# The first graph's column blocks and x ahead of the keys and the row loads in a four-layer graph network

## The chip, the cores and the metric

The kernel runs on one core of a Trainium2 chip. The metric is the device time of one execution, in microseconds (us), as the median of several executions. Five engines run side by side, each through its own list of instructions: TensorE (PE, matmuls and transposes), VectorE (DVE), ScalarE (ACT), GpSimd (POOL) and SyncE (SP, which here only issues transfers). ACT and POOL issue transfers as well. Engines wait for each other, and for transfers, by semaphores.

## The reference

Sixteen graphs of 1024 nodes with 64 features each go through four layers. `adj` is a dense 1024 x 1024 matrix for each graph with few non-zero entries. Each layer norms x, applies ReLU, and adds its result to x.

```python
# x (16, 1024, 64), adj (16, 1024, 1024), nodemask (16, 1024)
h = maximum(layernorm(x), 0)
x = x + einsum('bnf,of->bno', einsum('bnm,bmf->bnf', adj, h), L0_W)
h = maximum(layernorm(x), 0)
x = x + gru(relu(adj @ mlp(h)), h)                 # layer 1: message, then gates
h = maximum(layernorm(x), 0)
T1 = adj @ h; T2 = 2 * adj @ T1 - h                # layer 2: Chebyshev
x = x + (K0 * h + K1 * T1 + K2 * T2) @ weight + bias
h = maximum(layernorm(x), 0)
# layer 3: neighbours of each node from adj > 0, some dropped where there are more than ten;
# for each feature the 0.25, 0.5 and 0.75 quantiles over the neighbours, weighted 0.25, 0.5, 0.25
x = x + mlp2(h + quantiles(h, neighbours(adj))) * nodemask
```

## The kernel before, in words

Every graph passes these stages, each written as a Python generator that yields instructions:

- `transposing` (lines 798 to 832) loads the adjacency matrix by column blocks (128 columns, 512 KB each, eight a graph), transposes them on TensorE against the identity matrix and has ACT copy the result to a tile `AT`.
- `layers` (line 851) loads x of its graph into `pay`, and computes layers 0 to 2, with products `AT,nodes` on TensorE. Two such chains run at once, one for even graphs and one for odd. `norm` (line 834) is the layer norm: DVE sums a row (`st`), ACT squares (`sq`) and takes the root (`sd`), DVE forms `ri` and `off`, ACT writes the normed rows (`nodes`). At the end, `table` and `rows` are stored to DRAM (line 619).
- `lists` (line 633), called from `listing`, finds each node's neighbours from the matrix's rows, also eight loads of 512 KB a graph. For each it forms a `key` on DVE from the row and the constant `keys`, which lies in the tile `c16` (550 KB, loaded once from `half`), and takes the largest by MAX8 instructions.
- `gathering` and `gathers` fetch the neighbours' features by indirect transfers of POOL, 80 for a graph (line 613), and at the end those of nodes with long lists, which `longest` numbers (`whom`).
- `quantiling` sorts what was gathered on DVE, and `dense` is the last small network.

A planner, `Weave` (line 311), orders all of this when the program is built. It asks each generator for its next instruction, keeps a model of durations, takes the engine that can start earliest, and on it the instruction of lowest key among those that could start within 0.1 us. A bare number that a generator yields sets its key from there on. So x of graph 0 has key -1.0 (line 1039), and rows of graph 0 have key 0.0. The planned order is then fixed for every engine and for SP's issues. Where the model shows a gap of more than 0.5 us on TensorE, the planner puts fillers in it: matmuls of `ones` (line 567), whose result nobody reads. `leash` makes a gather wait for instructions of TensorE that the model has finished by then.

Ahead of the planned part stands a set-up in `Fast.__init__`: constants `c32` (with the identity matrix), the weights, small biases by POOL, and `wg`, two transposes of weights that DVE copies out of PSUM at line 535. The banks that the planned matmuls write are allotted after this set-up's PSUM pool.

For graph 0, blocks 2 to 7 and rows 2 to 5 go to parts of the tiles `G`, which are otherwise used by the gathers (`self.early`), so that all eight blocks and six rows have a place at the start.

Of the kernel before, what the change touches and what calls it, by code (L numbers as in the profile page):

```python
# [454 lines left out]
class Fast:  # L455
# [4 lines left out]
    def __init__(self, tc, half, whole, weights):  # L460
        self.tc, self.nc = tc, tc.nc
        (W0, W1, b1, W2, b2, Wih, bih, Whh, bhh, Wc, K, bc, M1, mb1, M2, mb2) = weights
        nc = self.nc
# [4 lines left out]
        def fixed(name, shape, dtype):  # L468
            return cp.tile(shape, dtype, name=name)
# [6 lines left out]
        c16 = fixed("c16", [P, half.shape[1]], F16)  # L476
# [15 lines left out]
        with tc.tile_pool(name="fsetup_ps", bufs=1, space=PSUM) as spp:  # L492
            passing = self.small("h1", (P, 512))
            w0 = passing[0:C, 0:C]
            nc.scalar.dma_start(w0, W0)
            whi = passing[0:96, C:C + 2 * P].rearrange("p (a g) -> p a g", a=2)
            nc.scalar.dma_start(whi[:, :, 0:C], Whh.rearrange("(a p) h -> p a h", p=96))
            nc.scalar.dma_start(whi[:, :, C:P], Wih.rearrange("(a p) h -> p a h", p=96))
            nc.scalar.dma_start(c16, half)
            self.kc = fixed("kc", [P, 3], F32)  # L500
            nc.gpsimd.dma_start(self.kc, K.rearrange("k o -> o k").to_broadcast([P, 3]))
            bi = fixed("bi", [P, 2], F32)
            nc.gpsimd.dma_start(bi[:, 0:1], bih[0:2 * C, None])
            nc.gpsimd.dma_start(bi[:, 1:2], bhh[0:2 * C, None])
            w0t_ps = spp.tile([C, C], F32, name="w0t_ps")
            nc.tensor.transpose(w0t_ps, w0, ident[:C, :C])
            self.w0t = fixed("w0t", [C, C], F32)
            nc.vector.tensor_copy(self.w0t, w0t_ps)

            self.w1 = fixed("w1", [C, C], F32)  # L510
            nc.gpsimd.dma_start(self.w1, W1)
            self.b1c = fixed("b1c", [C, 1], F32)
            nc.gpsimd.dma_start(self.b1c, b1[:, None])
            self.w2a = fixed("w2a", [C, C], F32)
            nc.gpsimd.dma_start(self.w2a, W2)
            self.b2r = fixed("b2r", [1, C], F32)
            nc.gpsimd.dma_start(self.b2r, b2[None, :])
            self.wca = fixed("wca", [C, C], F32)
            nc.gpsimd.dma_start(self.wca, Wc)
            self.bcr = fixed("bcr", [1, C], F32)  # L520
            nc.gpsimd.dma_start(self.bcr, bc[None, :])
            k02 = fixed("k02", [P, 1], F32)
            nc.vector.tensor_sub(k02, self.kc[:, 0:1], self.kc[:, 2:3])
            self.k02 = fixed("k02ident", [P, P], F32)
            nc.vector.tensor_scalar(self.k02, ident, k02, None, op0=ALU.mult)
            self.k22 = fixed("k22", [P, 1], F32)
            nc.vector.tensor_scalar(self.k22, self.kc[:, 2:3], 2.0, None, op0=ALU.mult)

            whi_ps = spp.tile([P, 2, 96], F32, name="whi_ps")
            for a in range(2):
                nc.tensor.transpose(whi_ps[:, a, :], whi[:, a, :], ident[:96, :96])
            self.wg = fixed("wg", [P, 3 * C], F32)
            nc.vector.tensor_copy(self.wg, whi_ps.rearrange("p a g -> p (a g)"))
            self.brz = fixed("brz", [P, 1], F32)
            nc.vector.tensor_add(self.brz, bi[:, 0:1], bi[:, 1:2])
            self.bin_ = fixed("bin", [C, 1], F32)
            nc.gpsimd.dma_start(self.bin_, bih[2 * C:3 * C, None])
            self.bhn = fixed("bhn", [C, 1], F32)  # L540
            nc.gpsimd.dma_start(self.bhn, bhh[2 * C:3 * C, None])

            self.m1 = fixed("m1", [C, P], F32)
            nc.gpsimd.dma_start(self.m1, M1)
            self.mb1c = fixed("mb1c", [P, 1], F32)
            nc.gpsimd.dma_start(self.mb1c, mb1[:, None])
            self.m2 = fixed("m2", [P, C], F32)
            nc.gpsimd.dma_start(self.m2, M2)
            self.mb2r = fixed("mb2r", [1, 4, C], F32)
            nc.gpsimd.dma_start(self.mb2r, mb2[None, None, :].to_broadcast([1, 4, C]))  # L550
# [82 lines left out]
    def lists(self, b, adj, nodemask):  # L633


        V, D = self.V, self.D
# [6 lines left out]
        def load(t):  # L643
            row = self.early.pop() if b == 0 and 2 <= t < 6 else (yield "row")
            yield D.dma_start(row, adj[b, t * P:(t + 1) * P, :])
            rows.append(row)

        yield from load(0)
        mu8 = self.small("mu8", (NT, P), U8)
        yield D.dma_start(mu8, nodemask[b, :].rearrange("(t p) -> t p", p=P))  # L650
# [147 lines left out]
    def transposing(self, adj):  # L798

        D, T, S = self.D, self.T, self.S  # L800
        blocks = {}


        early = self.early

        def load(i):
            b, j = divmod(i, NT)
            blocks[i] = block = early.pop(0).rearrange("p (t m) -> p t m", m=P) if 2 <= i < NT else (yield "block")
            yield D.dma_start(block, adj[b, :, j * P:(j + 1) * P].rearrange("(t p) m -> p t m", p=P))

        total = GRAPHS * NT
        yield -1.0
        for i in range(NT):
            if i == 4:
                yield 0.5
            yield from load(i)
        for i in range(total):
            b, j = divmod(i, NT)
            yield float(b) - 0.7
            if NT <= i + 1 < total:  # L820
                yield from load(i + 1)
            block = blocks.pop(i)
            at = yield "AT"
            for half in range(2):
                bank = yield "tp"
                for q in range(4):
                    yield T.transpose(bank[:, q * P:(q + 1) * P], block[:, 4 * half + q, :], self.ident)
                yield S.activation(at[:, 512 * half:512 * half + 512], bank, AF.Copy)
                self.weave.give("tp", bank)
            if not 2 <= i < NT:  # L830
                self.weave.give("block", block)
            self.turned[b].append(at)
# [1069 lines left out]
```

## Time and profile before

The time before is 2494.44 us, the median of three executions (2476.52, 2494.44, 2508.35).

| | |
|---|---|
| profiled execution: its own time | 2479.22 us |
| its span in the profile | 2477.4 us |
| mean granted TensorE clock | 0.882 |
| TensorE matmuls busy | 2168.9 us (88% of the span), 8704 |
| of these, fillers (line 567) | 676.4 us, 2705 |
| VectorE busy | 1796.3 us (73%) |
| ScalarE busy | 935.2 us (38%) |
| GpSimd busy | 1595.6 us (64%) |
| first and last store of a table | 147.1 us, 2038.9 us |
| first gather of graph 0, of graph 15 | 152.1 us, 2080.0 us |
| last gather issued | 2410.3 us |

Of the groups of instructions in the page, a line gives line, engine and operation, then output and input with their shapes and the count, then the busy time and the mean duration of one in ns, and behind the second bar the idle time of the engine just before these instructions and what ended most of it. Many instructions are recorded by a helper and all have line 288; they are told apart by their tiles. A line of a timeline has start, duration, engine, line, operation, tiles, count and, in brackets, the idle time before and its releaser. A matmul of 32-bit floats appears as two records. In the chain of waits, each piece is what the next piece was waiting for.

### The profile page before, as it was taken

To read this page: it belongs to the slowest core of one execution; us is meant where nothing else is said; L and a number is where in the kernel's file an instruction comes from. 1 tells how busy PE (TensorE), PEld (TensorE's weight loads), DVE (VectorE), ACT (ScalarE), POOL (GpSimd) and SP (SyncE) were. 2 spreads that over 40 slices of the span, in tenths; PEclk is the share of its full clock that TensorE was granted. 3 is DMA by queue.
4 is the path that set the end of the run, shared out by engine and by line. 5 is a ranking of instruction groups with operands and counts; after the bars stand their busy time and mean duration, and the time that the engine had idled before them with its cause. 6 is when DMAs were issued, how large, how long until landed. Compare 5 with 4: busy or idle time off the path is not lost.

```text
span 2477.4 us, 28435 instructions
## 1 busy us (share of the span) xinstructions
PE 2168.9 (88%) x8704; PEld 955.1 (39%) x8704; DVE 1796.3 (73%) x4505; ACT 935.2 (38%) x2714; POOL 1595.6 (64%) x1441
## 2 busy tenths in 40 slices
PE   8999899999898979897988898989898887779857
PEld 3344334343443333434342434342433333334414
DVE  5878687878696878787878877887777484447553
ACT  4444444354444353535353535353534211101000
POOL 1037676767675767676766676776676677777670
PEclk9999898889897989898989898999897887889969
DMA  6345526262626262616252525262522112121110
GB/s 211 111 112 155 115 65 136 57 138 64 121 74 137 56 160 49 149 39 155 56 133 53 139 65 134 60 146 49 140 38 36 23 35 27 23 28 29 23 24 5
DMA packets 265406, 208.68 MB, mean 84 GB/s; under 512 B 78208, under 2 KB 225984, under 8 KB 265248
## 3 DMA queue, kind: packets, MB, share of 16 engines
q1 hardware_dynamic: 218368, 157.32, 23.3%
q0 software_dynamic: 46096, 48.62, 13.0%
q8 instruction: 72, 1.18, 0.2%
q10 hardware_dynamic: 784, 0.86, 0.1%
q14 instruction: 86, 0.70, 0.1%
HBM read 187.51 MB, written 19.17 MB: 83 GB/s over the span
## 4 chain that ended last, share of the span: by engine, by line
PE 61%; DVE 14%; issue 7%; another core or an unknown queue 7%; ACT 7%; DMA 3%; POOL 1%; SPq 0%; ACTq 0%; DVEq 0%; POOLq 0%
PE bank L288 49%; PE bank L567 13%; DVE G L288 5%; DVE net L288 3%; ACT sq L288 2%; DVE cand L288 1%; DMA block<-in_adj 1%; ACT wide L288 1%; DVE hn L288 1%; DMA pay<-in_x 1%; ACT nodes L288 1%; ACT G L288 1%; DVE st L288 1%; DVE pay L288 1%
## 5 line engine op out<-in xcount | busy, mean ns | idle before, releaser
L613 POOL DMA_INDIRECT G<-table,pay x1402 | 1564.9, 1116 | 812.9 <-issue 374.3
L567 PE MATMUL bank<-ones 128*128 128x512 f16 x2705 | 676.4, 399 | 57.4 <-issue 55.7
L288 PE MATMUL bank<-AT,nodes 128*64 128x512 f32 x2048 | 645.9, 650 | 38.8 <-ACT nodes L288 21.2
L567 PEld LDWEIGHTS <-ones 128*128 128x128 f16 x2705 | 267.6, 102 | 412.6 <-issue 162.8
L288 PEld LDWEIGHTS bank<-AT,nodes 128*64 128x64 f32 x2048 | 171.5, 146 | 374.8 <-issue 286.3
L288 ACT ACTIVATE sq<-pay,st 128x64 f32<-128x64 f32 x512 | 177.1, 346 | 130.1 <-DVE st L288 65.5
L288 DVE MAX8 cand<-key 128x8 f16<-128x128 f16 x1024 | 214.4, 279 | 5.7 <-DVE key L288 2.1
L288 ACT ACTIVATE AT<-bank 128x512 f32<-128x512 f32 x256 | 148.3, 591 | 177.5 <-PE bank L288 131.1
L288 ACT ACTIVATE wide<-bank 64x512 f32<-64x512 f32 x128 | 75.6, 591 | 359.8 <-PE bank L288 253.6
L288 PE MATMUL bank<-c,block 128*128 128x128 f32 x976 | 185.7, 313 | 21.1 <-ACT AT L288 9.1
L288 DVE TENSOR_TENSOR G<-G 128x1024 f32<-128x1024 f32 (+7 forms) x215 | 187.2, 903 | 2.6
L288 PEld LDWEIGHTS bank<-c,block 128*128 128x128 f32 x976 | 127.5, 158 | 159.4 <-issue 135.5
L288 DVE SCALAR_TENSOR_TENSOR key<-row,c 128x1024 f16<-128x1024 f32 x124 | 150.2, 1211 | 38.0 <-DMA row<-in_adj 29.3
L288 PE MATMUL bank<-G,c 128*128 128x512 f32 (+3 forms) x382 | 165.0, 571 | 14.0 <-DVE G L288 7.1
L288 ACT ACTIVATE nodes<-pay,off,ri 128x64 f32<-128x64 f32 x384 | 148.8, 430 | 36.1 <-DVE off L288 15.8
L288 DVE TENSOR_TENSOR yo<-bank,pay 128x256 f32<-128x256 f32 (+2 forms) x36 | 14.8, 411 | 181.5 <-PE bank L288 97.6
L288 DVE TENSOR_TENSOR net<-G 128x1024 f32<-128x1024 f32 (+7 forms) x140 | 141.1, 1033 | 1.3
L288 ACT ACTIVATE G<-G,coef 128x64 f32<-128x64 f32 x384 | 93.8, 336 | 96.8 <-DVE coef L288 96.7
L288 DVE TENSOR_TENSOR G<-net 128x512 f32<-128x512 f32 (+12 forms) x123 | 110.2, 939 | 1.2
L288 DVE MAX8 L<-cand 128x8 f16<-128x64 f16 x384 | 87.4, 228 | 29.2 <-remote 9.7
L288 PE MATMUL bank<-wide,wg 64*64 64x512 f32 (+1 forms) x192 | 105.1, 628 | 3.6 <-ACT wide L288 3.4
L288 DVE TENSOR_TENSOR G<-G,net 128x1024 f32<-128x1024 f32 (+5 forms) x113 | 104.4, 960 | 1.4
(176 smaller groups left out, 2238.4 us busy)
## 6 DMA issues: line engine op xcount, KB each, us to landing
row<-in_adj SPq DMA_DIRECT2D x124, 512.0 KB
block<-in_adj SPq DMA_DIRECT2D x122, 512.0 KB
G<-table,pay POOLq DMA_INDIRECT x1402
rows<-pay SPq DMA_DIRECT2D x16, 632.0 KB
G<-in_adj SPq DMA_DIRECT2D x10, 512.0 KB
table<-pay SPq DMA_DIRECT2D x16, 264.0 KB
pay<-in_x SPq DMA_DIRECT2D x16, 256.0 KB
out<-yo SPq DMA_DIRECT2D x16, 256.0 KB
```

The costliest lines, as they stand in the source:

```text
L288: return Op(self, lambda: f(*args, **kwargs), writes, reads, cost, later)
L567: weave.spare = (self.T, lambda: nc.tensor.matmul(busy, ones[:, 0:P], ones[:, 0:512], start=True, stop=True), [busy], [ones], 0.22)
L613: return self.nc.gpsimd.indirect_dma_start(out=out, out_offset=None, in_=table, in_offset=bass.IndirectOffsetOnAxis(ap=at, axis=0))
```

## The change

x of graph 0 and all eight column blocks of graph 0 are asked for first, then the keys, then the matrix's rows.

- The generator `transposing` starts with key -0.9 instead of -1.0, so x of graph 0 (key -1.0) goes ahead of the blocks. The step that set its key to 0.5 ahead of the fifth block is removed, so blocks 4 to 7 keep -0.9 and go ahead of the rows.
- The load of `c16` is no longer issued by ACT in the set-up; the tile and its source are kept, and `lists` issues the load from SP ahead of the first row of graph 0.

```diff
@@ -496,7 +496,7 @@
             nc.scalar.dma_start(whi[:, :, 0:C], Whh.rearrange("(a p) h -> p a h", p=96))
             nc.scalar.dma_start(whi[:, :, C:P], Wih.rearrange("(a p) h -> p a h", p=96))
-            nc.scalar.dma_start(c16, half)
+            self.c16 = c16, half
             self.kc = fixed("kc", [P, 3], F32)
@@ -645,6 +645,8 @@
             yield D.dma_start(row, adj[b, t * P:(t + 1) * P, :])
             rows.append(row)
 
+        if b == 0:
+            yield D.dma_start(*self.c16)
         yield from load(0)
@@ -809,10 +811,8 @@
         total = GRAPHS * NT
-        yield -1.0
+        yield -0.9
         for i in range(NT):
-            if i == 4:
-                yield 0.5
             yield from load(i)
```

In the order that the built program has, SP's issues start like this, before and after (b is a column block, x the features, r a row, m the mask, K the keys; the second x is that of graph 1):

```text
before   b b b b x r m r r r r r b b b b r r b b x b b b b b b r m r ...
after    x b b b b b b b b K r m r r r r r r r b b x b b b b b r m r ...
```

## The prediction

> **What bounds the kernel now.** I read the page's groups first, then GpSimd's timeline, then the chain of waits over the first 60 us, then the vector engine's (DVE's) and ScalarE's (ACT's) timelines and the two-microsecond windows of that stretch.
>
> ```profile
> span 2477.4 us, 28435 instructions
> ...
> L613 POOL DMA_INDIRECT G<-table,pay x1402 | 1564.9, 1116 | 812.9 <-issue 374.3
> L567 PE MATMUL bank<-ones 128*128 128x512 f16 x2705 | 676.4, 399 | 57.4 <-issue 55.7
> ```
>
> GpSimd's timeline, first gathers (start, duration, idle before):
>
> ```profile
> 152.08 1.03 POOL L613 DMA_INDIRECT G<-table,pay  x1 [135.95 <-DMA table<-pay]
> 153.41 0.98 POOL L613 DMA_INDIRECT G<-table,pay  x1 [0.30 <-issue]
> ```
>
> From there the gathers of one graph follow those of the last with next to no hole: graph 1 begins at 279.5, graph 8 at 1185.9, graph 15 at 2080.0, and the first gather of the long rows at 2200.5. So the time is **152 us of start + 16 graphs of 128 us + 277 us of tail**. The table of graph 1 is stored at 250.4 and its gathers begin 29 us later, the lead being some 55 to 60 us from graph 5 on: no later gather waits for its table. A graph's 128 us are 80 gathers of 1.25 us (0.95 + 0.30 issue) = 100, some 13 for gathers over 0.95 us, and some 17 of longer holes, which name PE and ACT as releasers. TensorE is the second bound, 88% busy, with 2705 filler matmuls among its work.
>
> The edit reaches the first 152 us. The chain there:
>
> ```profile
> 2.41 7.23 DMA h<-in_L_gnn_W_ih
> 9.65 0.14 issue
> 9.78 0.57 PE whi_ps L533 x2
> 10.35 0.02 issue
> 10.37 0.37 DVE wg L535
> 10.74 0.04 issue
> 10.78 6.97 PE bank L567 x24
> 17.75 0.87 PE bank L288 x8
> 18.62 4.53 PE bank L567 x21
> 23.16 24.85 PE bank L288 x92
> ```
>
> Graph 0's first layer starts at 23.16, behind 45 fillers that TensorE may begin only when DVE has copied wg out of PSUM. Beside it, DVE and ACT:
>
> ```profile
> 7.40 0.16 DVE L523 TENSOR_TENSOR k<-kc 128x1 f32<-128x1 f32 x1 [5.81 <-DMA kc<-in_L_gnn_K]
> ...
> 14.91 0.69 DVE L288 TENSOR_REDUCE st<-pay 128x8 f32<-128x512 f32 x1 [4.18 <-DMA pay<-in_x]
> ...
> 16.64 1.23 DVE L288 SCALAR_TENSOR_TENSOR key<-row,c 128x1024 f16<-128x1024 f32 x1 [0.83 <-DMA row<-in_adj]
> ```
>
> ```profile
> 16.26 0.35 ACT L288 ACTIVATE sq<-pay,st 128x64 f32<-128x64 f32 x1
> ...
> 21.32 0.30 ACT L288 ACTIVATE sd<-va,eps 128x8 f32<-128x8 f32 x1
> ```
>
> x lands at 14.9, and ACT has the first normed rows (nodes) from 22.10: x and the fillers are ready nearly together.
>
> **What the Trainium skill says.** "DMA: Bandwidth & Descriptors", section "Issuing engines are not separate DMA queues": transfers of SP, ACT and GpSimd run on the same 16 engines, so moving the keys from ACT's queue to SP's buys no bandwidth, only a place in the line. The trace agrees: windows of 2 us between 10 and 34 us move 322 to 415 GB/s whichever queue issues, and from 36 to 48 us nothing moves, 11 MB having been loaded. "Perfetto Trace Analysis", section "Tensor Engine Instruction (MATMUL, LD_WEIGHTS)": ACT, DVE and GpSimd are strict FIFO. The trace agrees: DVE idles 9.24 us before the residual add at 50.97, with three MAX8 of the same row behind it.
>
> **The change, part by part.** I compared the order in which both built programs put each engine's instructions, and the semaphores that they wait for.
>
> 1. *x first, then eight blocks.* x is issued at 0.76 instead of 6.13. The nearest row for its landing is a later x: 5.03 us from issue to landing in the chain at 904.46. So some 5.8 instead of 14.9: 9 us earlier. Blocks follow at about 1.5 us each (0.524 MB at 350 GB/s); the first layer uses one in 3.1 us (24.85/8), so they aren't waited for, as in the kernel before.
>
> 2. *What this meets on DVE.* In the new order the sum st comes ahead of k, but its scaling stands behind k, which waits for kc until 7.40. Scaling ends at 7.82. From the first square to the end of off the trace has 22.07 - 16.26 = 5.81 (eight squares, the 1.28 table load, sd, ri, off), so off ends at 13.7. **The copy of wg now stands behind ri and off**, where it stood ahead of them: it ends at 14.05 instead of 10.74. TensorE's first filler waits for exactly that copy (its awaited DVE count rises from 10 to 14), and all its work queues behind. In the new order 26 fillers, 8 transposes, 13 fillers follow: 26 x 0.290 + 0.87 + 13 x 0.216 = 11.2. The first layer starts at 14.1 + 11.2 = 25.3: **2.1 us later**. Bounds: had wg stayed ahead, 22.0 (-1.2); were there no fillers, as soon as nodes is ready, 13.8 (-9.4); kc some 2 us later, +4.
>
> 3. *Keys and rows after the blocks.* Ahead of row 0's end lie c32, weights, x, eight blocks, keys and row 0: 0.18 + 0.11 + 0.26 + 4.19 + 0.56 + 0.52 = 5.8 MB, which the windows of before reach at 20 us. The first key starts at some 20.3 instead of 16.64. Before the residual add DVE now has four whole rows and seven MAX8 of the fifth, where it had five and five of the sixth: one row (4.25, from key to key) less two MAX8 (0.21) = 3.8 us go behind the add. With the 2.1 of step 2 the lists of graph 0 end 6 us later, about 69 instead of 63.2. Who waits: TensorE's transpose of the mask, queued ahead of the second matmul by w1; it costs about what it cost before (1.48), being one matmul later in the order. Then DVE had idle slots of 2.5 (row 8's transfer), 1.0 and 1.4 up to 85.4, which take the 3.8. Cover gone, it would reach the table in full. ACT loses one DMA issue (0.35, ahead of its first work: nothing). SP's issue order is changed, but each of these issues waits for a transfer eight places earlier, and these land well before. GpSimd's own order is unchanged.
> First gather: 152.1 + 2.1 + 0.4 = **154.6 (+2.5)**, from -9 (everything intended) to +7 (no slot takes the extra row).
>
> 4. *The order after that.* A planner orders all engines, so everything moves a little. Counted in the two orders: fillers 2673 instead of 2705; at 0.25 us (676.4/2705), with the chain spending 12.6% of the span in fillers that are busy 27.3%, 32 x 0.25 x 0.46 = -3.7. Gathers of the 16 graphs that wait on TensorE: 543 instead of 531; holes over 0.5 us sum to 278 us there (without the 136 at the start), 0.52 a wait: +6. From graph 8 to 13 the queue of SP before settles into a recurring pattern; the new order enters the same sequence four graphs earlier, with the same fillers per graph (89, 111, 89, 113, 86, 116, 93). Graphs 0 to 7 took 129.2 each, 8 to 15 126.8: 4 x 2.4 = -10. Each of these could be nothing or double. The last four graphs have a new pattern: +-8. The tail's gathers are the same ones in the same order: 0. The numbers for the long rows (whom) were ready at 2051 against 2200, and the lists of graph 15 end at the same place in DVE's order: still covered.
>
> Sum: +2.5 - 3.7 + 6 - 10 = **-5 us** against the profiled execution's 2479.2. That one lies 15 below the median of the runs shown (2494.44), so against the median: 2494 - 5 = 2489.
>
> **The rivals.** (a) *It does what it says*, and x leads: start -9, pattern -10, nothing lost: 2475. For it: x is waited for at 14.91. Against it: the filler's wait for wg. It can't pass 2% by the start alone (9.4 us is 0.4%). With holes halved besides (17 to 8 a graph, -140) it would be 2340; a third of that, 2430, is faster. (b) *Slower: the gathers' waits on TensorE.* Some 34 to 40 of a graph's 80 gathers wait for a place in TensorE's order. If the new interleaving lets TensorE lag, the holes grow from 17 to 21 us: 16 x 4 = +64, 2558. It decides from 3.1 us a graph (50/16). Against it: load per graph and waits per graph are counted nearly equal. (c) *Nothing moves*: wg's copy and x cancel, 2494.
>
> **How the numbers follow.** About 2% is what a measurement of this kernel can tell from no change (three runs span 1.3%), so the lines are at 2445 and 2544. My forecast with its own spread (2465 to 2515) 0.60, (c) 0.14, (a) 0.15 of which nearly all beyond 2% would come from holes, (b) 0.11. Range 2450 to 2525: bounds of start and pattern both ways, and part of (a) and (b). Faster 0.14, same 0.74, slower 0.12.
>
> **What would show it.** Right: st before kc, DVE's wg ending near 14, the first AT,nodes product near 25, first key near 20, first gather near 154.6, gathers of graph 15 ending at 2190 to 2210. Wrong: first gather before 148 (then wg or the fillers weren't the gate); holes before gathers above 20 us a graph; GpSimd waiting for a table store after graph 0.

## The result and the profile after

The changed kernel takes 2480.3 us (median of 20 executions, 2461.3 to 2499.2) against 2489.4 for the kernel before in the same comparison (20 executions). The ratio is **0.9967, 95% interval 0.9948 to 0.9987**: a gain of some 8 us, well inside the 2% that the prediction took for no change. The profiled execution of the changed kernel took 2493.43 us, so it is one of its long ones, while the profile of before (2479.22) was one of its short ones. Long executions have a low mean clock: the changed kernel's at 0.876, the profiled one among them, took 2483 to 2499 us, the one at 0.894 took 2461. The two profiles differ by +14 where the medians differ by -9. They are read below for places, not for the sum.

The page, with the same groups as before:

```profile
span 2491.2 us, 28387 instructions
...
L613 POOL DMA_INDIRECT G<-table,pay x1402 | 1566.6, 1117 | 822.0 <-issue 385.4
L567 PE MATMUL bank<-ones 128*128 128x512 f16 x2673 | 669.0, 401 | 42.3 <-issue 36.8
```

Gathers cost the same, there are 32 fillers fewer, and TensorE is as full as it was (2173.4 us busy). The start is what the edit touches directly. The chain of waits there (start, duration, what):

```profile
1.31 7.18 DMA kc<-in_L_gnn_K
...
14.49 0.17 DVE off L288
14.66 0.28 DVE wg L535
14.94 0.04 issue
14.98 7.27 PE bank L567 x26
22.25 0.87 PE bank L288 x8
23.12 2.81 PE bank L567 x13
25.93 24.85 PE bank L288 x92
```

The chain no longer begins with a load of weights, but with the small load of kc. Behind it come the squares, off, the copy of wg, the 39 fillers, and then the first layer at 25.93 instead of 23.16 (its first AT,nodes product at 26.19 instead of 23.41). DVE's timeline has the three loads that the edit was about, x, kc and the first row:

```profile
4.74 0.69 DVE L288 TENSOR_REDUCE st<-pay 128x8 f32<-128x512 f32 x1 [3.15 <-DMA pay<-in_x]
8.52 0.16 DVE L523 TENSOR_TENSOR k<-kc 128x1 f32<-128x1 f32 x1 [3.09 <-DMA kc<-in_L_gnn_K]
26.24 1.22 DVE L288 SCALAR_TENSOR_TENSOR key<-row,c 128x1024 f16<-128x1024 f32 x1 [11.31 <-DMA row<-in_adj]
```

x is there at 4.7 instead of 14.9, as asked. kc comes at 8.5 instead of 7.4, and the first row at 26.2 instead of 16.6. GpSimd's timeline:

```profile
160.34 1.03 POOL L613 DMA_INDIRECT G<-table,pay  x1 [143.09 <-PE bank L288]
```

The first gather is **8.3 us later** than before (152.08), and yet the median isn't higher. So between the first gather and the end something gives back more than 8 us, though not in these two profiles, in which 2325 and 2331 us follow the first gather. The experiments ask what the start costs, whether it carries to the end, and what gives it back.

### The profile page after: what moved, and what is told of

It reads as the page before. It is cut to its first block, busy times and chain, and to the rows that moved or that the text cites. A ratio compares the mean times of both kernels' runs of the same rounds, so it can differ in the third digit from the quotient of the medians.

```text
span 2491.2 us, 28387 instructions
## 1 busy us (share of the span) xinstructions
PE 2173.4 (87%) x8672; PEld 950.7 (38%) x8672; DVE 1795.7 (72%) x4505; ACT 935.3 (38%) x2714; POOL 1597.2 (64%) x1441
## 4 chain that ended last, share of the span: by engine, by line
PE 55%; DVE 17%; another core or an unknown queue 9%; issue 8%; ACT 8%; DMA 2%; POOL 0%; SPq 0%; DVEq 0%; POOLq 0%; ACTq 0%
PE bank L288 46%; PE bank L567 9%; DVE G L288 7%; DVE net L288 3%; ACT sq L288 3%; ACT G L288 2%; ACT wide L288 1%; DVE hn L288 1%; DVE cand L288 1%; DMA block<-in_adj 1%; DVE pay L288 1%; DVE key L288 1%; DVE st L288 1%; DMA G<-table,pay 1%
## 5 line engine op out<-in xcount | busy, mean ns | idle before, releaser
L567 PE MATMUL bank<-ones 128*128 128x512 f16 x2673 | 669.0, 401 | 42.3 <-issue 36.8
L288 PEld LDWEIGHTS bank<-AT,nodes 128*64 128x64 f32 x2048 | 164.5, 147 | 372.2 <-issue 306.4
L288 PE MATMUL bank<-c,block 128*128 128x128 f32 x976 | 192.7, 317 | 33.4 <-DMA block<-in_adj 12.2
L288 PE MATMUL bank<-G,c 128*128 128x512 f32 (+3 forms) x382 | 152.2, 539 | 14.3 <-issue 4.9
L288 ACT ACTIVATE nodes<-pay,off,ri 128x64 f32<-128x64 f32 x384 | 148.6, 430 | 39.9 <-DVE off L288 19.1
```

Of the source, the lines that this page charges most:

```text
L288: return Op(self, lambda: f(*args, **kwargs), writes, reads, cost, later)
L567: weave.spare = (self.T, lambda: nc.tensor.matmul(busy, ones[:, 0:P], ones[:, 0:512], start=True, stop=True), [busy], [ones], 0.22)
```

## The experiments

Each group of kernels ran on one chip beside the kernel before, and the chips differ: the kernel before takes 2291.2 us beside the first group, 2490.7 beside the second, 2453.8 beside the third and 2463.5 beside the last. So ratios are compared, not times. From here on, "old" and "new" interleaving mean the two orders that the planner finds from graph 1 on: that of the kernel before, and that of the changed one. Times of gathers are from one profile each (first gather; from there to the start of graph 8; from there to the first gather of the long rows).

| run | before | ratio (interval) | interleaving | first gather | graphs 0-7 | graphs 8-15 |
|---|---|---|---|---|---|---|
| before, changed | 2489 | 0.9967 (0.9948-0.9987) | old, new | 152.1, 160.3 | 1033.8, 1036.5 | 1014.6, 1015.5 |
| e_nofill | 2291 | 0.9919 (0.9894-0.9945) | new | 151.3 | 945.4 | 939.3 |
| e_wg | 2291 | 0.9951 (0.9937-0.9965) | new | 157.8 | 941.8 | 940.9 |
| e_c16 | 2291 | 1.0016 (0.9997-1.0035) | old | 158.8 | 950.6 | 932.1 |
| e_x | 2291 | 0.9922 (0.9898-0.9947) | new | 154.2 | 944.2 | 933.1 |
| r_after | 2491 | 0.9992 (0.9973-1.0011) | new | 161.8 | 1022.5 | 1018.3 |
| r_before | 2491 | 0.9997 (0.9969-1.0025) | old | 151.3 | 1046.8 | 1015.5 |
| e_fill2 | 2491 | 0.9991 (0.9966-1.0015) | new | 166.8 | 1030.1 | 1022.3 |
| e_best | 2491 | 0.9960 (0.9935-0.9985) | new | 152.0 | 1024.3 | 1014.3 |
| e_best2 | 2454 | 0.9918 (0.9894-0.9942) | new | 151.6 | 1014.0 | 997.1 |
| e_allfill | 2454 | 0.9939 (0.9913-0.9966) | new | 153.7 | 1029.6 | 1009.6 |
| e_noleash | 2454 | 1.4626 (1.4560-1.4692) | new | 148.6 | 1551.3 | 1519.7 |
| e_swap | 2464 | 0.9992 (0.9966-1.0018) | old | 155.4 | 1040.0 | 1020.8 |

### What gates the first layer: e_nofill and e_wg

e_nofill takes away the fillers ahead of graph 0's first layer, e_wg moves the copy of wg on DVE ahead of ri (`wg_copy` is the instruction that line 535 makes).

```diff
# e_nofill
-            if self.spare and line is self.spare[0]:
+            if self.spare and line is self.spare[0] and start > 14.0:
# e_wg
-        yield V.reciprocal(ri, sd)
+        self.weave.behind((yield V.reciprocal(ri, sd)), self.wg_copy)
```

> The changed kernel without the 39 fillers that stand ahead of graph 0's first layer; every other instruction of every engine keeps its order. Theory 1 (fillers gate the first layer, and the start carries to the end): first product AT,nodes at 16 to 17 instead of 25.93, the residual add at about 45.9 (where DVE's earlier queue ends) instead of 53.74, first gather near 152.5 instead of 160.34, median 8 below the changed kernel's 2480, so 2472. Rival A (the start is absorbed by the gather stream): first layer as early, but the median stays at 2480. Rival B (blocks, not fillers, gate): first layer's end moves by under 3, first gather stays at 158 or later.

> The changed kernel with one thing moved: DVE copies wg ahead of ri and off; every other engine's list is the same. Theory 1 (the prediction's step 2): first filler at about 10.8 instead of 14.98, the 26 and 13 fillers and 8 transposes as long as before, so the first layer at 21.7 instead of 25.93, residual add at 49.5, first gather at about 156, median 2476. Rival A: same start, median 2480. Rival C (kc, not wg's place, is late, so wg cannot go before 13): first filler after 13, nothing moves.

Without fillers the first AT,nodes product stands at 17.80, against 26.19 in the changed kernel. DVE's timeline of e_nofill:

```profile
45.74 0.69 DVE L288 TENSOR_TENSOR pay<-pay,bank 128x512 f32<-128x512 f32 x1 [1.03 <-PE bank L288]
```

The residual add is 8.0 earlier than in the changed kernel (53.74, where DVE idles 7.80 ahead of it), and now DVE has hardly any idle time left: a still earlier first layer would find DVE busy with keys. First gather: 151.3, against 160.3 in the changed kernel's profile. With wg ahead, its copy ends at 10.80, the first product is at 23.29, the add at 50.85 and the first gather at 157.8, each about 1.5 later than expected but in the order that was expected. So the prediction's gate is right: TensorE waits for wg's copy, then works off fillers. Rivals B and C of the expectations fall.

Whether the start carries to the end is less clear. The ratio of e_nofill is near theory 1 (2472 is a ratio of 0.993) and clear of rival A (2480 is 0.996), but the changed kernel didn't run on that chip. Between e_wg and e_nofill lie 6.5 us of first gather and 0.9951 - 0.9919 = 0.0032 of the time, 7.3 us, with intervals that overlap; e_x, below, begins its gathers 2.9 us after e_nofill and takes as long.

### The opposite: e_fill2

The changed kernel with the fillers at the start doubled.

```diff
-                for _ in range(int(FILL * gap / self.spare[4]) if gap > 0.5 else 0):
+                for _ in range(int(FILL * gap / self.spare[4]) * (2 if start < 14.0 else 1) if gap > 0.5 else 0):
```

> The changed kernel with twice as many fillers (78 instead of 39) ahead of graph 0's first layer; every other list keeps its order. Theory 1 (the start carries to the end one for one): first layer, residual add and first gather later by the length of 39 fillers, 39 x 0.22 to 0.29 = 8.6 to 11.3, so first gather near 169, and the median 8 to 11 above the changed kernel's. Rival A (absorbed by the gather stream): first gather as late, median within 3 of the changed kernel's.

The residual add is 8.0 later than in r_after (62.81 against 54.80), the first gather 5.0 later (166.8 against 161.8), and the time is the same: 0.9991 against 0.9992. That is a miss. The expected 8 to 11 us would be a ratio of 1.0024 or more, and the interval ends at 1.0015. On this slower chip 3 of the 8 us are absorbed before the first gather. The other 5 would be a ratio of 1.0012; they aren't seen at the end, but the interval doesn't exclude them. So that the start carries one for one is not shown.

### What the interleaving is worth: e_c16 and e_x

e_c16 is the changed kernel with the keys issued by ACT again. e_x is the kernel before with x alone moved to the front.

```diff
# e_c16, from the changed kernel
-            self.c16 = c16, half
+            nc.scalar.dma_start(c16, half)
...
-        if b == 0:
-            yield D.dma_start(*self.c16)
# e_x, from the kernel before
-        yield -1.0
+        yield -0.9
```

> The changed kernel with the keys still issued by ACT in the set-up (x and the eight blocks first, as in the change). The plan then has the interleaving of the kernel before from graph 1 on, and DVE's first key stands ahead of ri. Start: first key at 24 to 26, so ri at 26 to 28 and the first layer at 27 to 29, first gather 161 to 163. Theory 1 (the new interleaving is what gains, about 17 against a start that is 8 late): the changed kernel's 2480 + 2 + 17 = 2499. Rival A (start absorbed, interleaving gains 9): 2489. Rival D (the earlier loads themselves gain, interleaving does nothing): 2480 to 2483.

> The kernel before with only the key of the transposing step at -0.9: x first, then four blocks, the keys by ACT, rows, then the last four blocks. Its plan has the changed kernel's interleaving from graph 1 on, with the start's loads nearly as in the kernel before. Start: wg copied by 10.8, first layer near 22, first gather near 151. Theory 1 (new interleaving worth 17, start carries): 2489 - 1 - 17 = 2471. Rival A (interleaving worth 9, start absorbed): 2480. Rival D (asking for all eight blocks first is what gains): 2488.

e_c16 loads as the changed kernel does (first row at 26.56), begins its gathers at 158.8, 1.0 after e_wg, and has the old interleaving: 1.0016 against 0.9951, intervals apart. That is 0.0065 x 2291 = 15 us, less 1 for the start. Taken alone, e_c16's interval leaves theory 1 (2499 is a ratio of 1.004) just outside and admits rival A (2489 is 1.000). e_x has the new interleaving with only four blocks ahead of the rows: 0.9922, where theory 1 had it (2471 is 0.993), with rivals A (0.996) and D (0.999) outside its interval. So **asking for all eight blocks first isn't what gains**; the order of the planner is, and a single key changes it. The profiles of this group do not show the difference by themselves (first gather to long rows: 882.7 for e_wg and for e_c16); it is the medians that do.

### Both kernels side by side: r_after and r_before

The two kernels themselves, unchanged, on one chip.

> The changed kernel itself, on the chip and with the runs of the kernel before that the other three share. Theory 1: first gather at 158 to 161 in its profile, 6 to 8 behind the kernel before, and a ratio to it of 0.9967 (the ratio measured already), the gap of some 15 between the two made up between the first gather and the end by the other interleaving. Rival E (the sign of the difference belongs to one chip): a ratio of 1.000 or more.

> The kernel before itself, for a profile taken beside that of the changed kernel: first gather at 152, first key at 16.6, first layer at 23.2. Every theory: a ratio of 1.000 within its interval, which shows what the interval is worth.

The first gathers repeat: 161.8 and 151.3. What comes ahead of them repeats less well: in r_before x lands at 16.25 instead of 14.91, the first key is at 17.74 (expected 16.6) and the first AT,nodes product at 25.39 instead of 23.41, and still its first gather is 0.8 earlier. So differences of 1 to 2 us between single profiles say little. The ratio of the changed kernel is 0.9992 here, whose interval overlaps the first one's: the two measure a gain of 0.1 and 0.3%, and rival E is not excluded for a single chip. In the profiles of slow chips (the first pair and this group) graphs 0 to 7 take 1033.8 and 1046.8 in the old interleaving, mean 1040.3, and 1036.5, 1022.5, 1030.1 and 1024.3 in the new, mean 1028.4: **12 less, in the first eight graphs**, but with 13 and 14 us between the profiles of one interleaving. Graphs 8 to 15 take 1015.0 and 1017.6. Against each other at an equal first gather (151.3 and 152.0) stand r_before and e_best: 0.9997 against 0.9960, 9 us for the interleaving, though the intervals overlap a little. e_nofill and e_best2 begin their gathers as early as the kernel before does in its two profiles (151.3 and 151.6), and are 0.0081 and 0.0082 faster than it, 19 and 20 us; of the kernel before there is no profile on their chips.

### Where in the old interleaving: e_swap

In both timelines of SP the stores of graph 1's table stand near 249, and what follows differs. e_c16 (old):

```profile
249.11 0.57 SPq L619 DMA_DIRECT2D rows<-pay  x1
249.73 0.78 SPq L288 DMA_DIRECT2D pay<-in_x  x1
250.61 4.40 SPq L288 DMA_DIRECT2D row<-in_adj  x1
255.11 3.41 SPq L288 DMA_DIRECT2D block<-in_adj  x2
```

e_wg (new):

```profile
250.07 0.76 SPq L288 DMA_DIRECT2D pay<-in_x  x1
253.41 0.58 SPq L288 DMA_DIRECT2D block<-in_adj  x1
254.09 3.69 SPq L288 DMA_DIRECT2D row<-in_adj  x1
```

In the old one a row holds the head of SP's queue for 4.40, with two blocks behind it. TensorE in the stretch from 255 to 265 (length, then busy time and count of TensorE, weight loads, DVE, ACT and GpSimd; clock, DMA share, GB/s), first e_c16:

```profile
255.00:265.00 10.00, 2.18 (x9) 0.78 (x9) 4.25 (x16) 3.02 (x13) 2.85 (x4) 0.79 1.05 165
```

then e_wg:

```profile
255.00:265.00 10.00, 6.63 (x31) 3.10 (x29) 5.41 (x21) 6.36 (x25) 6.63 (x7) 0.86 1.10 155
```

TensorE starves, and GpSimd's gather at 269.00 in e_c16 idles 10.24 for TensorE. The holes at the same place in the two profiles of the kernel before are 8.31 and 7.36. e_swap exchanges the row and the block in e_c16, and nothing else (`held` is SP, `sent` counts what it has issued).

```diff
-            heads = [c for c in self.chains if c["op"]]
+            sent = self.sent
+            heads = [c for c in self.chains if c["op"] and not (c["gen"].__name__ == "listing" and c["op"].line is self.held and sent == 73)]
...
+            self.sent += line is self.held
```

> The kernel with x and the eight blocks first and the keys still by ACT (old interleaving), with a single exchange in SP's list: behind the stores of graph 1's table and rows and x of graph 3, a block is issued ahead of the row instead of behind it, as the new interleaving has it. Every other engine's order is the same. Theory 1 (the old interleaving's long hole before the gathers near 265 to 270 comes from this block): TensorE's wait for block there (4.6 to 5.2 without the exchange) goes, the hole of 7.4 to 10.2 shrinks to 5 or less, the period of graph 0's gathers is 4 to 6 shorter. The whole would then gain at most 0.2 per cent, less than an interval is wide. Rival I (TensorE waits there for nodes, thus for DVE, which waits for the row): the wait for block is replaced by a longer one for nodes, and the hole stays at 7 or more.

TensorE's wait for a block there is gone, and the hole is still 8.80 (gather at 271.40). TensorE now loses its time in fillers, with idle times of 1.72, 1.72 and 2.42 before them that nothing in the profile explains, then 16 fillers in 5.71; only then come transposes of a block, and the gather after them. Such idle times don't occur in e_c16's stretch, which was taken on another chip. A longer wait for nodes, as rival I has it, isn't there either. So this one block is not the cause, or not alone. **Which of the many exchanged instructions makes the new interleaving faster stays open.**

### What gained, joined: e_best and e_best2

e_best joins what gained: x first as in e_x, no fillers at the start, and the first key held behind off. e_best2 moves the three instructions on kc (lines 523 to 527, now made by a function `late`) behind off as well.

```diff
# e_best, from e_x, with the filler condition of e_nofill
         yield V.tensor_mul(off, st, ri)
+        self.normed = True
...
             A = rows[t]
+            yield lambda: hasattr(self, "normed")
# e_best2, from e_best
-        yield V.tensor_mul(off, st, ri)
+        made = yield V.tensor_mul(off, st, ri)
+        if not hasattr(self, "normed"):
+            for k in self.late():
+                self.weave.behind(k, made)
```

> The kernel before with x's load first (transposing's key -0.9, the last four blocks still after the rows, keys by ACT), no fillers ahead of the first layer, and the first key held behind off. Plan from graph 1 on as in the changed kernel. Theory 1: kc at 6.7, off at 12.7, first AT,nodes product at 15 to 16, residual add near 43.5 (106 before the first gather, as in the other runs), first gather near 150; ratio to the kernel before 0.990 to 0.991, the fastest so far. Rival B (the last four blocks, now behind six rows, are late for so early a layer): TensorE waits for block, add at 47 or later, ratio 0.992 as with x first alone.

> x first alone, no fillers at the start, first key behind off (the fastest so far), and now the three instructions on kc behind off too, so that the scaling of st no longer stands behind the wait for kc. Theory 1 (the prediction's step 2 had the mechanism, kc's landing was the mis-sized term): st scaled at 5.6 instead of 9.2, off at 11.5 instead of 15.0, first product 3.5 earlier (14.6 instead of 18.2), first gather 3 earlier, near 149; ratio to the kernel before 0.3 x 2490/100 lower at most, 0.992 to 0.995. Rival: bi or w0t, next in DVE's order ahead of ri, land as late as kc, and off moves by under 1.

e_best gains, 0.9960, but less than expected. kc landed at 9.06 in it, not at 6.7 as in e_x, off ended at 15.2 and the first product stands at 18.16. TensorE doesn't wait for a block in its first layer, so rival B falls. In e_best2 off is done at 12.1, close to the expectation, but what then decides is the copy of wg: it took 2.87 us (12.44 to 15.31) where it takes 0.36 elsewhere, and the first product is at 18.01. The product k02ident, which the edit moved to the place ahead of it, took 3.07 us instead of 0.28 and ended with it; why both are long isn't known. So kc's wait was removed and the start did not move (first gather 151.6 against 152.0). 0.9918 is the lowest ratio of all runs, within the intervals of e_nofill and e_x, and on another chip than e_best.

### Pacing and fillers: e_noleash and e_allfill

Rival (b) of the prediction feared the gathers' waits on TensorE. e_noleash is e_best without these added waits; e_allfill is e_best with no filler at all.

```diff
# e_noleash
-            if done:
-                self.after(ins, done[-1])
# e_allfill
-            if self.spare and line is self.spare[0] and start > 14.0:
+            if False:
```

> The same kernel as the fastest so far, without the extra waits of gathers on TensorE (the leash): gathers wait for their table, their buffer and nothing else; every engine's order is unchanged. What a gather's wait for a place in TensorE's order costs: theory 1 (the stream of gathers bounds the time, and its holes on this plan are such waits): holes over 0.5 us of graphs 1 to 15 fall from 256 to under 80, and the median falls by 100 or more where the holes were 256, by up to 30 where they were 45. Rival F (the gathers then only run up to the next table, because TensorE and DVE set the tables' pace): holes move to waits for table, median within 20 of the same kernel with the leash. Rival G (gathers bunch and crowd out block loads): slower by 20 or more.

> The same kernel as the fastest so far without any filler (0 instead of 2634); every other instruction keeps its order. Theory 1 (a filler fills time in which TensorE has nothing, but it runs in order and takes 0.25 to 0.41 where the plan has 0.22, so a run of them makes the next real work late): holes of the gathers shrink and the median falls by 10 to 60. Rival H (TensorE's matmuls are slower without fillers): a 64x512 product AT,nodes over 0.70 us on average instead of 0.65, median higher by 20 or more.

Without the added waits the kernel takes **3591.0 us, a ratio of 1.4626 (1.456 to 1.4692)**. All theories missed this. G has the sign, but not the size, and not the mechanism: from 200 to 2000 TensorE waits for blocks for 8.5 us in all. The gathers of a graph run back to back at 0.95 plus 0.30 us, and meanwhile the others stop. Windows of e_noleash, columns as above:

```profile
360.00:380.00 20.00, 10.25 (x27) 5.34 (x26) 6.99 (x33) 2.96 (x6) 15.43 (x16) 0.50 0.22 54
380.00:400.00 20.00, 0.00 (x0) 0.00 (x0) 4.78 (x15) 0.00 (x0) 15.13 (x16) 0.50 0.15 26
400.00:420.00 20.00, 0.00 (x0) 0.00 (x0) 3.61 (x4) 0.00 (x0) 15.42 (x16) 0.50 0.21 25
```

For 40 us neither TensorE nor ACT executes anything, and of all transfers only gathers move. TensorE's waits from 200 to 2000 (total, times, longest):

```profile
PE bank L288 <- issue: 492.9, 40, 57.5
```

"issue" is time in which the engine waited for nothing that the profile shows. The profile does not say what it is. That gathers follow one another without a hole isn't enough to bring it on. In e_best2, on the same chip and with the added waits, 65 gathers do so from 1311 to 1407, none but the first after more than 0.5 us of idle time, and TensorE is 90% busy (columns as above):

```profile
1311.30:1407.20 95.90, 86.08 (x396) 42.55 (x396) 83.50 (x207) 48.84 (x151) 76.32 (x65) 0.89 0.49 115
```

In e_wg 396 do so from 419 to 996, with TensorE 93% busy. So the run shows that taking the added waits out brings the stops, and not by what means.

Without fillers nothing is lost and nothing gained: 0.9939, its interval overlapping that of e_best2 on the same chip. The mean granted clock falls from 0.888 to 0.746. The Trainium skill, "TensorE: Matmul & The Clock Gate", section "What's actually happening", says that the throttled clock is the default and activity releases it; the two mean clocks agree with that. But the AT,nodes products get slower by 7% only. The groups by shape of e_allfill (busy time, mean ns, then idle time ahead and its releasers):

```profile
L288 PE MATMUL bank<-AT,nodes 128*64 128x512 f32 x2048 | 681.9, 691 | 162.3 <-ACT nodes L288 121.6 <-issue 22.5 <-DVE nodes L288 7.4
```

The same group of e_best2, with its fillers:

```profile
L288 PE MATMUL bank<-AT,nodes 128*64 128x512 f32 x2048 | 637.8, 643 | 56.0 <-issue 33.7 <-ACT nodes L288 15.8 <-ACT sq L288 2.7
```

The holes over 0.5 us in graphs 1 to 15 don't shrink (240 us, with fillers 224), and the median is 2439 against 2436. So theory 1 is wrong on both counts. Rival H is right that the products are slower, though short of its 0.70 us, and wrong that the time is longer.

## Why the prediction was right, and where it was not

The forecast was 2489 against a median of 2494, a gain of 5; measured are 9 and, repeated, 4.5. It was right that the change is worth little and that the planner's order is worth more than the loads. That the sum fits is in part luck: the start came out 6 to 8 us worse than forecast, and the order behind it better by about as much or more.

- **Step 1, x lands at 5.8.** Measured 4.7.
- **Step 2, the gate.** Right: the scaling of the sum st is delayed by kc, wg's copy stands behind off, fillers follow. First layer at 25.3 predicted, 25.93 measured. The mis-sized term is kc: 8.49 instead of 7.40, and it varies: 6.66 in e_x and 9.06 in e_best, whose transfers start in the same order. e_wg and e_nofill confirm the two places where time was to be had.
- **Step 3, the first key at 20.3.** Wrong by 6: 26.24. The 5.8 MB ahead of it were priced at the rate of the old order. In the windows of the first 20 us the old order moved 203 and 378 GB/s (198 and 312 in r_before), the new one 181 and 263 (197 and 250 in r_after). This error cost nothing, because DVE still idled 7.80 before the add and the lists ended at 69.9 (predicted 69).
- **Step 3, "DVE had idle slots ... which take the 3.8".** This term failed, and with it the forecast of the first gather: 154.6, bounded by +7; it came at 160.3 and 161.8. At the end of the lists DVE is 6.7 us later than before (69.9 against 63.2). At its last key ahead of the second residual add, with the same instructions done, it is still 5.2 later (136.42 against 131.20), so the slots took 1.5 us. Between r_before and r_after they took nothing: 5.7 later at the end of the lists, 8.9 at that key. The second add itself, for which DVE has no idle time left, is 3.9 later.
- **What step 3 left out: the other order also acts ahead of the first gather.** From the second residual add to the third the changed kernel needs 2.5 us more. The second and third add of the kernel before, then of the changed kernel, then of e_x:

```profile
134.60 0.68 DVE L288 TENSOR_TENSOR pay<-pay,bank 128x512 f32<-128x512 f32 x1
138.86 0.69 DVE L288 TENSOR_TENSOR pay<-pay,bank 128x512 f32<-128x512 f32 x1 [1.71 <-PE bank L288]
```

```profile
138.46 0.67 DVE L288 TENSOR_TENSOR pay<-pay,bank 128x512 f32<-128x512 f32 x1
145.22 0.69 DVE L288 TENSOR_TENSOR pay<-pay,bank 128x512 f32<-128x512 f32 x1 [2.86 <-PE bank L288]
```

```profile
133.85 0.69 DVE L288 TENSOR_TENSOR pay<-pay,bank 128x512 f32<-128x512 f32 x1 [1.01 <-PE bank L288]
141.12 0.69 DVE L288 TENSOR_TENSOR pay<-pay,bank 128x512 f32<-128x512 f32 x1 [3.36 <-PE bank L288]
```

The third add waits for TensorE's products with w0t. In the new order one more AT,nodes product and six more transposes stand ahead of them. e_x has its first row at 15.93 and its lists end 2 us earlier than in the kernel before, so no late row is at work there, and it has the same 7 us between these adds. From the first add to the first gather it needs 106.4 us, like the changed kernel (106.6), where the kernel before needs 101.1 and 98.4 in its two profiles, and e_c16 and e_swap, with late rows and the old order, 103.9 and 102.8. By these figures both the late rows and the other order make the first gather later; how much belongs to each, single profiles can't tell. Behind the third add, the table's store is issued 5.4 us later than before, and 2.9 more are added between it and the first gather, for which the profile names TensorE and not the table as the last to be waited for.
- **Step 4, the order after that.** Predicted -3.7 for fillers, +6 for gathers' waits, -10 for the pattern entered earlier, together -7.7. Measured on slow chips, from first gather to long rows: -12 in graphs 0 to 7, +2.6 in graphs 8 to 15, together -9.4. That is two profiles against four, and in the first eight graphs those of one interleaving lie up to 14 us apart, so it is a size and not a proof. The ratios put it at 9 to 20: 9 from e_best, 14 from e_c16 against e_wg, 19 and 20 from e_nofill and e_best2. The gathers of graph 15 end at 2212 and 2203, at the edge of the 2190 to 2210 that were forecast. The prediction expected the gain in the first eight graphs. The profiles of the slow chips put it there, within their scatter; between e_wg and e_c16 on the fast chip, 8.8 us less in graphs 0 to 7 are lost again in graphs 8 to 15. Its parts can't be told apart, and its cause inside the order is not shown (e_swap).
- **The rivals.** (a), x leads: the first gather was not earlier. (b), TensorE lets the holes grow: 252.5 us in graphs 1 to 15 after, 253.6 before. (c), wg and x cancel: the start was worse than that.

## What to carry to other kernels

Moving a load to the front pays only as far as the next thing in each engine's order allows: here x came 10 us earlier and the first layer 3 us later, since small waits (kc) and a copy (wg) stood ahead of it and fillers behind. Where a planner orders everything, a small edit also buys another order; compare versions that share the order before crediting the edit itself. And cover is to be shown at the end of the path, not at its beginning: of 3.8 us of work that was to go into idle slots, 1.5 did so in one pair of profiles and nothing in the other.

## What the runs showed of the hardware

- With the gathers' added waits on TensorE taken out, TensorE executes nothing for up to 57.5 us at a time, for no reason that the profile shows, and the kernel takes 46% longer than the kernel before. An unbroken row of gathers alone doesn't do this: 396 in a row in e_wg left TensorE 93% busy.
- The kernel before takes 2291 to 2491 us on different chips. Most of such a difference lies between the gathers: holes over 0.5 us in graphs 1 to 15 sum to 38.0 in e_wg on the fastest chip and to 258.5 in r_after, nearly the same kernel, on a slow one, a difference of 220 where the spans differ by 198. TensorE's unexplained "issue" waits from 200 to 1800 are 0.2 us in the former and 42.2 in the latter.
- 2634 fillers raise the mean clock from 0.746 to 0.888, and the time doesn't change by more than the intervals (ratios 0.9939 without them, 0.9918 with them).
